# The last feed-forward pass of a fused float32 transformer block: gate and up from parts of 12 significant bits

## The chip, the cores and the metric

The kernel runs on one core of a Trainium2 chip. A core has a matrix engine (TensorE, PE in the profile, with its weight loads as PEld), a vector engine (VectorE, DVE), an activation engine (ScalarE, ACT), a programmable engine (GpSimd, POOL) and a queue engine that here only starts transfers (SyncE, SP). Each engine works through its own instructions strictly in order and waits on semaphores for the others. [...] The metric is the device time of one execution in microseconds (us), the median over runs.

## The reference

Four sequences of 512 rows with 256 features go through a windowed attention, a feed-forward layer, a causal attention and the same feed-forward layer again, each with a residual sum and a row normalization ahead of it. What matters here is the feed-forward layer, whose weights are stored as 4-bit codes with a scale for every 32 of them:

```python
Wg = dequant_nvfp4(gate_W_packed, gate_scales)   # 2048 x 256
Wu = dequant_nvfp4(up_W_packed, up_scales)       # 2048 x 256
Wd = dequant_nvfp4(down_W_packed, down_scales)   # 256 x 2048
gate = jnp.einsum('th,nh->tn', xt, Wg)
up = jnp.einsum('th,nh->tn', xt, Wu)
gelu = jnp.tanh(0.7978845608028654 * (gate + 0.044715 * gate ** 3)) * gate * 0.5 + gate * 0.5
out = jnp.einsum('tn,hn->th', gelu * up, Wd)
...
x = x + attn_a(layernorm(x))
x = x + ffn(layernorm(x))
x = x + attn_b(layernorm(x))
x = x + ffn(layernorm(x))
```

## The kernel before, in words

Everything is float32. The weights are unpacked once, early, and stay in SBUF: `Wf["g"]`, `Wf["u"]` and `Wf["d"]`, each as 2 x 4 tiles of 128 x 512. Index `par` picks the even or odd features (the contraction of 256 is done as two of 128), `q` a quarter of the 2048 hidden units.

A feed-forward pass (`ffn`, from line 891) serves one sequence `b`: 512 columns of activations in `xT` (128 x 2 x 512). It goes through two halves of eight hidden tiles each. For hidden tile n it makes the gate (two matmuls into a PSUM bank `pg`, line 903), on ACT the gelu of it into `gs` (line 915 for passes that use the gelu table, lines 909 to 913 and 930 to 931 for passes beside attention, which build it from a tanh), the up (two matmuls into `pu`, line 924), and on DVE their product `it` (line 935). After eight tiles the down product follows: four row groups `po`, each of eight matmuls over the eight `it` tiles (line 949), and on DVE the sum into the residual `X` (line 964). In the last pass each row group of the second half goes out by DMA (line 971). `pg`, `pu` and `po` share three PSUM banks (pool `fbank`), taken in turn.

There are eight passes, four of the first layer (names ending in f and a digit) and four of the second (s and a digit). `weave` puts the matmuls of a pass by hand between the matmuls of the attention that runs beside it: PE's order is the order written, `tc.manual_schedule(engines=PE_ONLY)`. The order of the instructions on ACT, DVE and POOL isn't written out; the framework's scheduler settles it when the program is built, from its own estimate of when each can run and from the order in which they were created. The pass of sequence 2 (`s2`) is the last with attention beside it. The pass of sequence 3 (`s3`) runs alone at the end of the kernel:

```python
weave(passes(), beside_causal(), 1.0)
weave(ffn(f1, i1, 3, got2[3], "s3", False, True), iter(()), 1.0)
```

Its input `got2[3]` comes from `norm_rows` (line 826): statistics of each row group on DVE (`bn_stats` and `bn_aggr` into `mv`, lines 838 and 839), the inverse root `rs` in two small POOL instructions (`inv_root`, lines 92 and 93: a multiply-add and a power), the normalized rows `xn` on DVE (line 856), eight transposes on PE into `xTp` (line 876), and one ACT copy of 128 x 1024 into `xT` (line 882). In PE's order these eight transposes lie inside the down product of `s2`, after ten of the 32 matmuls of its second half; the other 22 come behind them, and then the gate of `s3`.

The causal attention's tiles lie in four pools (`bc`, `b1`, `b2`, `b4`) that stay open to the end. The last thing the attention does is on POOL: the sum of its output rows into `X` (line 1221).

Of the kernel before, what the change touches and what calls it, by code (L numbers as in the profile page):

```python
# [10 lines left out]
F32 = mybir.dt.float32  # L11
F16 = mybir.dt.float16
I32 = mybir.dt.int32
AF = mybir.ActivationFunctionType
ALU = mybir.AluOpType
AX = mybir.AxisListType

P = 128
B, H, W = 4, 512, 256
# [3 lines left out]
NH = MLP // P  # L23
EPS = 1e-5
MASK = -1e30


def bcast(ap, axis, n):
# [7 lines left out]
def hybrid_kernel(  # L36
# [25 lines left out]
    nc = tc.nc  # L62
# [4 lines left out]
    side = ctx.enter_context(tc.tile_pool(name="ps2", bufs=2, space=bass.MemoryType.PSUM))  # L67
# [818 lines left out]
    def behind_due(ins):  # L886

        if "due" in state:
            queue_behind(ins, state["due"])

    def ffn(pool, ipool, b, xT, name, tanh, last, later=None):
        for half in range(2):
            inter = []
            for n in range(8 * half, 8 * half + 8):
                q, o = n // 4, (n % 4) * P
                if later:
                    later.room()
                    later.want(f"g{q}")
                pg = fbank.tile([P, 512], F32, tag="ps", name=f"pg_{name}_{n}")
                for par in range(2):  # L900
                    if par:
                        yield
                    nc.tensor.matmul(  # L903
                        pg, Wf["g"][par][q][:, o : o + P], xT[:, par, :], start=par == 0, stop=par == 1
                    )
                gs = pool.tile([P, 512], F32, tag="gs", name=f"gs_{name}_{n}")
                if tanh:

                    nc.scalar.copy(gs, pg)  # L909
                    g2 = pool.tile([P, 512], F32, tag="g2", name=f"g2_{name}_{n}")  # L910
                    nc.scalar.activation(g2, gs, AF.Square, scale=0.044715 ** 0.5)  # L911
                    nc.vector.scalar_tensor_tensor(g2, g2, 1.0, gs, ALU.add, ALU.mult)  # L912
                    nc.scalar.activation(g2, g2, AF.Tanh, scale=0.7978845608028654)
                else:
                    nc.scalar.activation(gs, pg, AF.Gelu_apprx_tanh)  # L915
                yield
                if later:
                    later.room()
                    later.want(f"u{q}")
                pu = fbank.tile([P, 512], F32, tag="ps", name=f"pu_{name}_{n}")  # L920
                for par in range(2):
                    if par:
                        yield
                    nc.tensor.matmul(  # L924
                        pu, Wf["u"][par][q][:, o : o + P], xT[:, par, :], start=par == 0, stop=par == 1
                    )
                it = ipool.tile([P, 512], F32, tag="it", name=f"it_{name}_{n}")
                if tanh:
                    gu = pool.tile([P, 512], F32, tag="gu", name=f"gu_{name}_{n}")
                    nc.vector.scalar_tensor_tensor(gu, pu, 0.5, gs, ALU.mult, ALU.mult)  # L930
                    nc.vector.scalar_tensor_tensor(it, g2, 1.0, gu, ALU.add, ALU.mult)
                elif later:
                    later.push(lambda it=it, pu=pu, gs=gs: nc.vector.tensor_tensor(it, pu, gs, ALU.mult), 1.3, 0.6)
                else:
                    behind_due(nc.vector.tensor_tensor(it, pu, gs, ALU.mult))
                inter.append(it)
                yield
            for i in range(4):
                if later:
                    later.room()  # L940
                po = fbank.tile([P, 512], F32, tag="ps", name=f"po_{name}_{half}_{i}")
                for k in range(8):
                    if later and i == 0 and k == 6:
                        later.room(0)
                    if later and i == 0 and k % 4 == 0:
                        later.want(f"d{2 * half + k // 4}")
                    n = 8 * half + k
                    j, par = n // 2, n % 2
                    nc.tensor.matmul(  # L949
                        po[:, 0:W],  # L950
                        inter[k][:, i * P : (i + 1) * P],
                        Wf["d"][par][j // 2][:, (j % 2) * W : (j % 2 + 1) * W],
                        start=k == 0,
                        stop=k == 7,
                    )
                    if k % 2:
                        yield

                parts = 2 if b == B - 1 and last and half == 1 and i == 3 else 1
                for n in range(parts):  # L960
                    at = slice(n * W // parts, (n + 1) * W // parts)

                    def put(i=i, at=at, po=po):
                        return nc.vector.tensor_tensor(X[b][:, i, at], po[:, at], X[b][:, i, at], ALU.add)  # L964

                    if later:
                        later.push(put, 0.4, 0.35)
                    else:
                        behind_due(put())
                    if last and half == 1:  # L970
                        (nc.scalar if n else nc.sync).dma_start(
                            out=out[b, i * P : (i + 1) * P, at], in_=X[b][:, i, at]
                        )

    def causal_consts(bc, c):

# [307 lines left out]
    def weave(main, work, share):  # L1287

        with tc.manual_schedule(engines=PE_ONLY):
            owed = 0.0  # L1290
            for w in work:
                owed += w * share
                while owed >= 0.86:
                    owed -= 0.86
                    next(main, None)
            for _ in main:
                pass
# [305 lines left out]
        for b in range(1, 3):  # L1603
            weave(ffn(f1, i1, b, got[b], f"f{b}", False, False), beside_window(b + 1), 1.0)

    bc = ctx.enter_context(tc.tile_pool(name="bc", bufs=1, side="left"))
    cc, got2 = {}, []

    def passes():
# [4 lines left out]

    def beside_causal():
        yield from causal_consts(bc, cc)
        b1 = ctx.enter_context(tc.tile_pool(name="b1", bufs=1, side="left"))
        b2 = ctx.enter_context(tc.tile_pool(name="b2", bufs=2, side="left"))
        b4 = ctx.enter_context(tc.tile_pool(name="b4", bufs=4, side="left"))
        other = norm_rows(f1, 1, "b1", mine, 5.0, True)  # L1620
        for b in range(B):

            work = scaled(causal_attention(b1, b2, b4, cc, b, mine[b]), 0.8 if b == 0 else 1.045)
            yield from amid(work, other)
            other = causal_end(b)
        yield from other

    weave(passes(), beside_causal(), 1.0)
    weave(ffn(f1, i1, 3, got2[3], "s3", False, True), iter(()), 1.0)


# [86 lines left out]
```

## Time and profile before

| what | value |
|---|---|
| time of the kernel | 1019.37 us median of 3 runs (1018.01 to 1022.12) |
| span of the profiled execution, first to last instruction | 1018.9 us |
| PE busy | 998.9 us, 98% of the span |
| DVE, ACT, POOL busy | 671.3, 351.0, 129.2 us |
| gate of `s3` begins on PE | 932.83 us |
| down of the second half of `s3` begins on PE | 1001.57 us |
| last sums into `X` begin on DVE | 1015.59 us |

No device time is given for the profiled execution by itself; its span is 0.47 us under the median, and inside the three runs. Times in the views are counted in us from the first instruction. A float32 matmul of 128 x 512 leaves two records on PE, so that "x4" in a line of the last pass is the two matmuls of one gate or up tile. The mean length of one such record overlaps the next; the distance from start to start is the true pace. A releaser, as in "<-DVE xn", is what ended the idle time ahead of an instruction.

### The profile page before, as it was taken

The numbers are of one execution on the slowest core, as the hardware profiler recorded it, in microseconds if no ns is written. First come the engines' busy times: TensorE is split into PE (matmuls) and PEld (weight loads), VectorE is DVE, ScalarE is ACT, GpSimd is POOL, SyncE is SP. The second block draws the span as 40 slices with busy tenths as digits, with TensorE's granted clock in tenths as the row PEclk, the third lists the DMA queues.
The fourth block names the chain that finished last, engine by engine and source line by source line (L and its number), as shares of the span: only waits on it lengthen the run. The fifth ranks groups of instructions, "written<-read, shape, count | busy, mean of one in ns | idle before, by whom it ended". The sixth has DMA issues, their size and how long they took to land.

```text
span 1018.9 us, 14266 instructions
## 1 busy us (share of the span) xinstructions
PE 998.9 (98%) x5552; PEld 589.2 (58%) x5552; DVE 671.3 (66%) x1581; ACT 351.0 (34%) x607; POOL 129.2 (13%) x251
## 2 busy tenths in 40 slices
PE   8989998999999999999999999999999999999998
PEld 6864657465746575554574644754645746446556
DVE  8889997987938678756577554766466575652111
ACT  3462142132112223435424346145253253451110
POOL 2100000100000013012330112401113201120000
PEclk9999999999999999999999999999999999999999
DMA  5220100000000020000000000000000000000000
GB/s 157 76 64 22 62 22 13 10 1 1 1 1 1 1 68 1 1 1 1 2 1 0 2 1 1 6 16 1 1 1 1 22 0 2 1 1 21 0 1 21
DMA packets 14900, 15.32 MB, mean 15 GB/s; under 512 B 2866, under 2 KB 11338, under 8 KB 14802
## 3 DMA queue, kind: packets, MB, share of 16 engines
q1 hardware_dynamic: 12416, 13.31, 4.4%
q10 hardware_dynamic: 2322, 1.07, 0.4%
q8 instruction: 43, 0.70, 0.3%
q14 instruction: 23, 0.19, 0.1%
q0 software_dynamic: 96, 0.05, 0.0%
HBM read 12.32 MB, written 2.10 MB: 14 GB/s over the span
## 4 chain that ended last, share of the span: by engine, by line
PE 91%; DVE 5%; ACT 1%; DMA 1%; issue 1%; POOL 0%; SPq 0%; POOLq 0%; DVEq 0%
PE pg_s L903 11%; PE pu_s L924 11%; PE po_s L949 11%; PE pg_f L903 10%; PE pu_f L924 10%; PE po_f L949 10%; PE s L1113 5%; PE o L1198 4%; PE sT L1162 4%; PE qkv_b L1052 3%; PE va L486 2%; PE qkT L1089 1%; PE qkv_b L1056 1%; PE zp L751 1%; PE sc L486 1%; PE ob L1213 1%
## 5 line engine op out<-in xcount | busy, mean ns | idle before, releaser
L1128 DVE CUSTOM_DVE_ANT_0 junk<-s,mask 128x512 f32<-128x512 f32 (+3 forms) x256 | 110.2, 487 | 36.8 <-PE s L1113 19.8
L903 PE MATMUL pg_s<-xT_s,g 128*128 128x512 f32 x256 | 126.7, 603 | 0.0
L924 PE MATMUL pu_s<-xT_s,u 128*128 128x512 f32 x256 | 125.4, 601 | 0.0
L903 PE MATMUL pg_f<-xT_f,g 128*128 128x512 f32 x256 | 123.8, 598 | 0.7 <-ACT xT_f L879 0.7
L924 PE MATMUL pu_f<-xT_f,u 128*128 128x512 f32 x256 | 122.5, 595 | 0.0
L949 PE MATMUL po_s<-d,it_s 128*128 128x256 f32 x512 | 118.0, 382 | 0.0
L949 PE MATMUL po_f<-d,it_f 128*128 128x256 f32 x512 | 117.4, 382 | 0.4 <-DVE d L820 0.4
L949 PEld LDWEIGHTS po_s<-d,it_s 128*128 128x128 f32 x512 | 95.2, 190 | 20.8 <-issue 8.8
L949 PEld LDWEIGHTS po_f<-d,it_f 128*128 128x128 f32 x512 | 95.1, 190 | 18.4 <-issue 5.4
L1178 POOL TENSOR_SCALAR_AFFINE_SELECT e<-e 128x256 f32<-128x256 f32 x128 | 52.5, 422 | 345.2 <-ACT e L1174 342.5
L1174 ACT ACTIVATE e<-sT 128x1024 f32<-128x1024 f32 (+1 forms) x72 | 66.4, 968 | 72.0 <-PE sT L1162 72.0
L924 PEld LDWEIGHTS pu_f<-xT_f,u 128*128 128x128 f32 x256 | 47.3, 190 | 55.0 <-issue 53.0
L903 PEld LDWEIGHTS pg_s<-xT_s,g 128*128 128x128 f32 x256 | 46.0, 190 | 56.8 <-issue 50.9
L915 ACT ACTIVATE gs_f<-pg_f 128x512 f32<-128x512 f32 x48 | 28.6, 596 | 142.2 <-PE pg_f L903 136.5
L924 PEld LDWEIGHTS pu_s<-xT_s,u 128*128 128x128 f32 x256 | 46.1, 190 | 54.4 <-issue 50.2
L903 PEld LDWEIGHTS pg_f<-xT_f,g 128*128 128x128 f32 x256 | 46.8, 190 | 52.8 <-issue 48.1
L912 DVE SCALAR_TENSOR_TENSOR g_s<-g_s,gs_s 128x512 f32<-128x512 f32 x48 | 33.2, 691 | 59.0 <-ACT g_s L911 58.5
L909 ACT COPY gs_s<-pg_s 128x512 f32<-128x512 f32 x48 | 28.1, 586 | 67.8 <-PE pg_s L903 67.6
L1113 PE MATMUL s<-kT,qT 16*128 16x384 f32 (+3 forms) x512 | 50.0, 467 | 0.0
L964 DVE TENSOR_TENSOR X<-po_s,X 128x256 f32<-128x256 f32 (+1 forms) x33 | 13.5, 413 | 54.0 <-PE po_s L949 54.0
L1198 PE MATMUL o<-e,V 128*32 128x256 f32 (+3 forms) x512 | 44.4, 441 | 0.4 <-PE sT L1162 0.4
L1113 PEld LDWEIGHTS s<-kT,qT 16*128 16x128 f32 x512 | 23.1, 183 | 32.5 <-issue 11.6
(241 smaller groups left out, 1348.2 us busy)
## 6 DMA issues: line engine op xcount, KB each, us to landing
X<-in_x_dram SPq DMA_DIRECT2D x4, 512.0 KB
out_dram<-X SPq DMA_DIRECT2D x15, 128.0 KB
xa<-in_x_dram SPq DMA_DIRECT2D x28, 64.0 KB
pkg<-in_gate_p_dram SPq DMA_DIRECT2D x4, 256.0 KB
sbg<-in_gate_s_dram SPq DMA_DIRECT2D x4, 256.0 KB
pku<-in_up_p_dram SPq DMA_DIRECT2D x4, 256.0 KB
sbu<-in_up_s_dram SPq DMA_DIRECT2D x4, 256.0 KB
pkd<-in_down_p_dram SPq DMA_DIRECT2D x4, 256.0 KB
```

The lines of the kernel that those rows point to most:

```text
L486: nc.tensor.matmul(dst, ident, part, start=n == 0 and not onto, stop=n == len(parts) - 1, skip_group_check=onto)
L903: nc.tensor.matmul(pg, Wf["g"][par][q][:, o : o + P], xT[:, par, :], start=par == 0, stop=par == 1)
L912: nc.vector.scalar_tensor_tensor(g2, g2, 1.0, gs, ALU.add, ALU.mult)
L924: nc.tensor.matmul(pu, Wf["u"][par][q][:, o : o + P], xT[:, par, :], start=par == 0, stop=par == 1)
L949: nc.tensor.matmul(po[:, 0:W], inter[k][:, i * P : (i + 1) * P], Wf["d"][par][j // 2][:, (j % 2) * W : (j % 2 + 1) * W], start=k == 0, sto ...
L1052: nc.tensor.matmul(ps[:, 0, :], xT[:, par, rows], c["wqk"][:, :, par], start=par == 0, stop=par == 1)
L1113: nc.tensor.matmul(pss[hl // 2][:, hl % 2, at : at + n], qT[h0 : h0 + HD, g, i * P : (i + 1) * P], kT[h0 : h0 + HD, g, 0:n], start=True, s ...
L1128: nc.vector.tensor_tensor_reduce(out=junk[:, 0:n], in0=pss[k][:, hl % 2, at : at + n], in1=c["mask"][:, 512 - n : 512], scale=1.0, scalar= ...
L1162: nc.tensor.matmul(pss[hl // 2][:, hl % 2, at : at + n], kT[h0 : h0 + HD + 1, g, kt * P : (kt + 1) * P], qT[h0 : h0 + HD + 1, g, kt * P : ...
L1174: nc.scalar.activation(e[:, :, 0 : 512 - at0], pss[k][:, :, at0:512], AF.Exp)
L1178: nc.gpsimd.affine_select(out=diag, in_=diag, pattern=[[0, 2], [1, P]], compare_op=ALU.is_ge, fill=0.0, base=0, channel_multiplier=-1,)
L1198: nc.tensor.matmul(outs[g][h0 : h0 + 32, kt * P : 512], v[:, kt, 4 * g + hl, :], e[:, hl % 2, at : at + n], start=kt == 0, stop=kt == 2,)
```

## The change

In the last pass gate and up are no longer float32 matmuls. Each operand is cut into a top part of 12 significant bits and a remainder, w = w0 + w1 and x = x0 + x1, and held as float32r, the float32 form that by the change's own description PE multiplies in a single pass where float32 takes four. The product needs four terms; the kernel gets them from three products. With s = 2^-12 it sums w0 x0 + w1 (4096 x1), scales that sum by 1 + s in PSUM, and adds (w1 - s w0)(x0 - 4096 x1); written out, this leaves w0 x0 + w0 x1 + w1 x0 + w1 x1. `in_parts` makes the three forms of the activations and `weight_parts` the three forms of each of the 16 gate and up weight tiles:

- activations, per `par`: two ACT instructions (the top part by a rounding scale `NEAR`, and 4096 x) and two DVE instructions
- weights, per tile: the top part on ACT, one form on DVE, the remainder on POOL

The 16 weight triples share 12 buffers, so that those of the last quarter (q = 3) wait until those of the first are used up. All of this lies in a new pool `alone`, which takes the room of the four attention pools; these are closed first.

`ffn_in_parts` replaces `ffn` for `s3`. `begin` does four float32r matmuls into a bank and then scales the bank in place on ACT by 1 + 2^-12; `end` adds two more float32r matmuls to the scaled bank. Between a tile's `begin` and its `end` PE does the `begin` of the next tile. Gelu, product and down (`down`, the old loop moved into a function of its own, line 949 now 956) are as before.

```diff
+F32R = mybir.dt.float32r
+STEP = 2.0 ** -12
+NEAR = 1.0 - 2.0 ** -13
...
+    def in_parts(pool, xT, name):
+
+        x4 = pool.tile([P, 2, 512], F32, name=f"x4_{name}")
+        xs = pool.tile([P, 3, 2, 512], F32R, name=f"xs_{name}")
+        for par in range(2):
+            nc.scalar.activation(xs[:, 0, par], xT[:, par], AF.Copy, scale=NEAR)
+            nc.scalar.activation(x4[:, par], xT[:, par], AF.Copy, scale=4096.0)
+        top = xs.bitcast(F32)
+        for par in range(2):
+            nc.vector.scalar_tensor_tensor(xs[:, 1, par], top[:, 0, par], -4096.0, x4[:, par], ALU.mult, ALU.add)
+            nc.vector.scalar_tensor_tensor(xs[:, 2, par], top[:, 0, par], 4097.0, x4[:, par], ALU.mult, ALU.subtract)
+        return xs
+
+    def weight_parts(pool):
+
+        parts = {}
+        for q in range(4):
+            for mat in ("g", "u"):
+                for par in range(2):
+                    w = Wf[mat][par][q]
+                    t = pool.tile([P, 3, 512], F32R, tag="parts", bufs=12, name=f"w{mat}{par}_{q}")
+                    top = t[:, 0].bitcast(F32)
+                    nc.scalar.activation(t[:, 0], w, AF.Copy, scale=NEAR)
+                    nc.vector.scalar_tensor_tensor(t[:, 2], top, -1.0 - STEP, w, ALU.mult, ALU.add)
+                    nc.gpsimd.tensor_tensor(t[:, 1], w, top, ALU.subtract)
+                    parts[mat, par, q] = t
+        return parts
+
+    def ffn_in_parts(pool, ipool, b, xs, parts, name, last):
+
+        def begin(mat, n):
+            q, o = n // 4, (n % 4) * P
+            ps = fbank.tile([P, 512], F32, tag="ps", name=f"p{mat}_{name}_{n}")
+            for k, (form, par) in enumerate(((0, 0), (0, 1), (1, 0), (1, 1))):
+                nc.tensor.matmul(
+                    ps, parts[mat, par, q][:, form, o : o + P], xs[:, form, par],
+                    start=k == 0, stop=k == 3,
+                )
+            nc.scalar.activation(ps, ps, AF.Copy, scale=1.0 + STEP)
+            return ps
+
+        def end(mat, n, ps):
+            q, o = n // 4, (n % 4) * P
+            for par in range(2):
+                nc.tensor.matmul(
+                    ps, parts[mat, par, q][:, 2, o : o + P], xs[:, 2, par],
+                    start=False, stop=par == 1, skip_group_check=True,
+                )
+            return ps
+
+        for half in range(2):
+            inter, gates, open_ = [], {}, None
+
+            def close():
+                mat, n, ps = open_
+                end(mat, n, ps)
+                if mat == "g":
+                    gs = gates[n] = pool.tile([P, 512], F32, tag="gs", name=f"gs_{name}_{n}")
+                    nc.scalar.activation(gs, ps, AF.Gelu_apprx_tanh)
+                else:
+                    it = ipool.tile([P, 512], F32, tag="it", name=f"it_{name}_{n}")
+                    nc.vector.tensor_tensor(it, ps, gates[n], ALU.mult)
+                    inter.append(it)
+
+            for n in range(8 * half, 8 * half + 8):
+                for mat in ("g", "u"):
+                    ps = begin(mat, n)
+                    yield 0.87
+                    if open_:
+                        close()
+                        yield 0.44
+                    open_ = mat, n, ps
+            close()
+            yield 0.44
+            for _ in down(b, name, half, inter, last):
+                yield 0.87
...
-    bc = ctx.enter_context(tc.tile_pool(name="bc", bufs=1, side="left"))
+    causal = ExitStack()
+    bc = causal.enter_context(tc.tile_pool(name="bc", bufs=1, side="left"))
...
     weave(passes(), beside_causal(), 1.0)
-    weave(ffn(f1, i1, 3, got2[3], "s3", False, True), iter(()), 1.0)
+    causal.close()
+    alone = ctx.enter_context(tc.tile_pool(name="alone", bufs=1, side="left"))
+    xs = in_parts(alone, got2[3], "s3")
+    weave(ffn_in_parts(f1, i1, 3, xs, weight_parts(alone), "s3", True), iter(()), 1.0)
```

In the changed program as built the queues around the start of `s3` run as follows (index of the quarter behind the name; "top" the ACT part of a weight tile, "form" its DVE part, "rest" its POOL part):

```
ACT   tanh of s2's last tile | 12 tops (q 0 to 2) | xT copy | 2 + 2 for x | scale g0 | scale u0 | gelu table load | gelu 0 | scale g1 | scale u1 | gelu 1 ...
      ... scale u3 | tops g q3 x2 | gelu 3 | tops u q3 x2 | scale g4 | scale u4 | gelu 4 ...
DVE   it 15 of s2 | statistics | form g0 | last statistics | form g0 | X sum | xn x4 | forms u0 x2, g1 x2, u1 x2 | X sum | 4 for x | form g2 | X sum | forms g2, u2 x2 | X sum | it 0 ...
POOL  X sum of the attention | rests g0 x2, u0 x2, g1 x1 | rs multiply-add | rest g1 | rs power | rests u1 x2, g2 x2, u2 x2 | rests q3 x4
PE    ... s2 down: 10 matmuls | 8 transposes | 22 matmuls | s3: begin g0, begin u0, end g0, begin g1, end u0, begin u1, end g1 ...
```

More of the change, by code (lines that the diff above doesn't have):

```diff
@@ L937, in ffn @@
                 yield
-            for i in range(4):
-                if later:
[L940 to L954, printed above, removed]
-                    )
[L956 to L973, printed above, removed]
@@ new lines, in ffn, with down, put @@
+            yield from down(b, name, half, inter, last, later)
+    def down(b, name, half, inter, last, later=None):
+        for i in range(4):
+            if later:
+                later.room()
+            po = fbank.tile([P, 512], F32, tag="ps", name=f"po_{name}_{half}_{i}")
+            for k in range(8):
+                if later and i == 0 and k == 6:
+                    later.room(0)
+                if later and i == 0 and k % 4 == 0:
+                    later.want(f"d{2 * half + k // 4}")
+                n = 8 * half + k
+                j, par = n // 2, n % 2
+                nc.tensor.matmul(
+                    po[:, 0:W],
+                    inter[k][:, i * P : (i + 1) * P],
+                    Wf["d"][par][j // 2][:, (j % 2) * W : (j % 2 + 1) * W],
+                    start=k == 0,
+                    stop=k == 7,
+                )
+                if k % 2:
+                    yield
+            parts = 2 if b == B - 1 and last and half == 1 and i == 3 else 1
+            for n in range(parts):
+                at = slice(n * W // parts, (n + 1) * W // parts)
+                def put(i=i, at=at, po=po):
+                    return nc.vector.tensor_tensor(X[b][:, i, at], po[:, at], X[b][:, i, at], ALU.add)
+                if later:
+                    later.push(put, 0.4, 0.35)
+                else:
+                    behind_due(put())
+                if last and half == 1:
+                    (nc.scalar if n else nc.sync).dma_start(
+                        out=out[b, i * P : (i + 1) * P, at], in_=X[b][:, i, at]
+                    )
@@ new lines, in ffn_in_parts @@
+    def ffn_in_parts(pool, ipool, b, xs, parts, name, last):
[12 more added lines that the diff above has]
+            for par in range(2):
+                nc.tensor.matmul(
+                    ps, parts[mat, par, q][:, 2, o : o + P], xs[:, 2, par],
+                    start=False, stop=par == 1, skip_group_check=True,
+                )
+            return ps
[7 more added lines that the diff above has]
+                    nc.scalar.activation(gs, ps, AF.Gelu_apprx_tanh)
+                else:
+                    it = ipool.tile([P, 512], F32, tag="it", name=f"it_{name}_{n}")
[13 more added lines that the diff above has]
+                yield 0.87
@@ L1616, in beside_causal @@
         yield from causal_consts(bc, cc)
-        b1 = ctx.enter_context(tc.tile_pool(name="b1", bufs=1, side="left"))
-        b2 = ctx.enter_context(tc.tile_pool(name="b2", bufs=2, side="left"))
-        b4 = ctx.enter_context(tc.tile_pool(name="b4", bufs=4, side="left"))
+        b1 = causal.enter_context(tc.tile_pool(name="b1", bufs=1, side="left"))
+        b2 = causal.enter_context(tc.tile_pool(name="b2", bufs=2, side="left"))
+        b4 = causal.enter_context(tc.tile_pool(name="b4", bufs=4, side="left"))
         other = norm_rows(f1, 1, "b1", mine, 5.0, True)
```

## The prediction

> **What bounds the kernel now.** I read the chain that ended last first. PE carries nearly all of it:
>
> ```profile
> PE 91%; DVE 5%; ACT 1%; DMA 1%; issue 1%; POOL 0%; SPq 0%; POOLq 0%; DVEq 0%
> ```
>
> Then its pieces in order of time around the start of the last pass (start, length, what):
>
> ```profile
> 917.08 0.74 POOL X L1221
> 917.84 0.75 DVE st_s L838 x2
> ...
> 919.98 0.23 DVE mv_s L839 x2
> 920.28 0.19 POOL rs_s L92
> 920.52 1.07 POOLq L1714
> 921.62 0.42 DVE xn_s L856
> 922.08 1.41 PE xTp_s L876 x8
> 923.49 9.50 PE po_s L949 x44
> 932.99 1.72 PE pg_s L903 x4
> 934.71 1.72 PE pu_s L924 x4
> ```
>
> Two things are to be seen. From 932.99 on, gate and up tiles follow each other every 1.72 us with nothing between: that stretch is PE's alone. And just before it the chain leaves PE: the normalization of sequence 3 goes through two small POOL instructions (the multiply-add and the power of the inverse root, 920.28 to 921.58), and PE's transposes hang on it. PE's order is fixed, so the 22 down matmuls behind the transposes (923.49, 9.50 us) wait as well. That the chain passes through POOL there costs 0.76 us of idle PE, as the timeline says in brackets:
>
> ```profile
> 920.56 1.02 POOL L93 TENSOR_TENSOR rs_s<-rs_s,mhalf 128x4 f32<-128x4 f32 x1
> ...
> 922.08 1.41 PE L876 MATMUL xTp_s<-ident,xn_s 128*128 128x128 f32 x8 [0.76 <-DVE xn_s L856]
> ...
> 924.56 1.28 ACT L915 ACT_TABLE_LOAD   x1
> ```
>
> Last, prices: the instructions of the tile `turned` (min/median/max in ns), and groups by form (busy us, mean ns).
>
> ```profile
> L1071 POOL TENSOR_TENSOR turned<-qb,rt x64: 449/632/645, 385.7 to 800.1; 128x128 f32<-128x128 f32 x64
> ```
>
> ```profile
> L1221 POOL TENSOR_TENSOR X<-X,on 128x256 f32<-128x256 f32 x16 | 11.7, 729 | 32.3 <-DVE on L1219 32.2
> ...
> L911 ACT ACTIVATE g_s<-gs_s 128x512 f32<-128x512 f32 x48 | 30.2, 630 | 1.5
> ...
> L909 ACT COPY gs_s<-pg_s 128x512 f32<-128x512 f32 x48 | 28.1, 586 | 67.8 <-PE pg_s L903 67.6
> ```
>
> **Part 1: fewer passes on PE.** A tile was four records of 0.429 us (1.72). A tile is now six matmuls of 512 columns. No row shows a float32r matmul. The upper bound is the record as it is, 0.429; the lower is half of it, 0.216, since a record of two float32 matmuls' four is two passes. I take 0.216, because the down product shows that PE and its weight loads can keep that pace: 64 records with a new 128 x 128 weight each (its load 0.19) in 13.81 us. So 6 x 0.216 = 1.295 a tile, 0.422 less, and over 32 tiles 13.5 us less.
>
> **Part 2: new waits in the loop.** From the queue order shown above, with 0.20 us from the last column on PE to ACT's start (934.54 to 934.74), 0.60 for a scale or gelu of 128 x 512, and 0.1 back to PE:
> - steady state: a tile's scale is ready 0.9 us after its `begin`, and PE is busy with others for 1.295 until its `end`. ACT's three instructions per n take 1.8 of 2.59 us, DVE's product 0.69. Three banks suffice by some 0.2 us. Nothing is lost. A scale in PSUM in place has no row; between 0.5 and 0.8 us it moves the sum by -0.6 to +1.3.
> - the last `end` of each half has only 0.43 us of cover: 0.49 lost, twice. The first `end` of each half: 0.06, twice.
> - the gelu table load (1.28) lay under s2's down product. Now it stands in ACT's queue behind the scales of tile 0, gelu 0 comes 1.28 later, and `begin` of up 1 needs its bank: 1.04 lost.
> - after n = 3, four tops of 0.63 for q 3 stand between the scales on ACT, two ahead of gelu 3 and two ahead of scale g4: `begin` u4 waits 1.1 for the bank, `end` g4 1.06 for its scale.
>
> Together 4.3 us, so the pass from its first gate to its end gains 13.5 - 4.3 = 9.2 us.
>
> **Part 3: the pass starts later.** This is where the change pays. Five rests are queued on POOL ahead of the multiply-add and a sixth ahead of the power; behind those two stand xn, the transposes, the 22 down matmuls and the whole last pass. The first top can't be used before POOL's sum into X ends (917.81): top at 917.9 to 918.5, first rest at 918.6. A rest of 128 x 512: from 449 ns at 128 columns (the shortest, undisturbed) to 729 at 256 is 2.19 ns a column, so 1.29 us. The bounds are 1.0 (a line from the 468 ns of a POOL product of 128 x 8 through the 729) and 1.46 (twice 729); I take the steeper line, being nearest in shape. Five are 6.45. Beside them DVE runs three instructions with two SBUF inputs (it 15 and two forms); such company stretches POOL from 449 to the median 632, a factor 1.41, over some 3 us: 0.9 more, 925.95. Multiply-add 0.28, rest 1.29, power 1.0: 928.5 where it was 921.58, 6.9 us later. PE, out of work since 921.35, starts the transposes at 929.0 instead of 922.08.
>
> PE has then been idle 7.7 us, and such a gap has a second price. Windows of 1 us show what thin work did early in this run (PE busy 72% of the window 36 to 37, 0.69 us of it idle before; the granted clock is the number after POOL's count):
>
> ```profile
> 38.00:39.00 1.00, 1.00 (x4) 0.74 (x3) 0.97 (x2) 0.00 (x0) 0.92 (x2) 0.50 0.00 0
> 39.00:40.00 1.00, 1.00 (x4) 0.82 (x3) 1.00 (x2) 0.00 (x0) 1.00 (x1) 0.50 0.00 0
> ```
>
> Half clock from about 37.3 to 40.7, so 3.4 us at half speed: 1.6 us lost here. Bounds: nothing, and 2.2 by the 4.36 us that the kernel's very first 20 records took at half pace. [...]
>
> The rest of the preparation hides. The transposes (1.24 us, at half clock 2.5) end at 931.5, their result is on ACT at 931.7; xT copy 1.01 and four ACT parts of 0.63: 935.2. On DVE six forms come first (0.61 apart, stretched by 1.6 beside POOL, as the DVE sum beside `turned` is, 672 ns against 426: to about 935.9), a sum into X, then four parts of x: 939.6. POOL's twelfth rest ends at 938.7. The down product covers all this: it ends at 931.5 + 9.5 + 0.5 (what is left of the half clock's 3.4 us) = 941.5. Without the clock's loss it would end at 939.9, with 0.3 us of cover left. So gate g0 starts at 941.5 against 932.83: 8.6 later. SP's transfers of sequence 2 follow its X sums and are as late; nobody waits for them.
>
> [...]
>
> **Sum.** 1018.9 (the profiled execution's span) - 9.2 + 8.6 = 1018.3. The median of the runs shown is 0.47 above that span: **1018.8 us**, within 0.5% of before (5.1 us, about what a measurement of this kernel can tell from no change). The rest of the kernel is issued as before: the other engines' queues are the same up to s2's last tile.
>
> **Rivals.**
> - *A short delay, faster.* POOL's rests take 1.0 us and don't suffer from DVE, and the clock holds: start 4.4 later, a scale of 0.5 in PSUM: -9.8 + 4.4, 1014.0. For it: the small products' flat line. Against: the 449 and 632. If the root did not wait for the rests at all, the parts of x would set the start, 1.0 late: 1011.2; the queue order speaks against it.
> - *A long delay, slower or the same.* Rests of 1.46 with full blocking and a clock loss of 2.2: POOL's and DVE's forms run one by one, the parts of x come at 944.6 and set the start, 11.9 late: 1022.1. A rest has to take some 2.2 us to pass 1024.5; a POOL path that is slow for float32r output could do that, and no row has one.
> - *The single pass isn't one, slower.* If a float32r matmul costs more than 0.245, 192 of them eat 5.7 us more and the kernel is slower by over 0.5%; at 0.24 it is 1023.4. At 0.429 the pass is 28.1 longer than before, 1056. For it: no row of such a matmul; against: the pace of the down product's loads.
>
> **How the numbers follow.** The balanced case, with its rests between 1.1 and 1.5 and the clock lost or not (1015.5 to 1022), 0.62. Short delay or better, under 1014.3: 0.15. Long delay beyond 1024.5: 0.13. Not a single pass: 0.10, half of it near the threshold. Hence faster 0.15, same 0.62, slower 0.23. The range leaves out a tenth below and a tenth above: 1013.5 to 1025.
>
> **What would show it.** Right: float32r records 0.216 apart; POOL's power ending about 928.5, and PE idle some 7 us ahead of the transposes with a granted clock near 0.5 after them; first gate at about 941.5; from there to the end 77 us against 86; stalls of about 1 us at up 1, twice at tile 4. Wrong: a rest well off 1.3 us, a clock that holds, a pace other than 0.216, or parts of x that arrive behind the down product.

## The result, and the profile after

The changed kernel takes 1025.72 us in the median of 5 runs (1025.27 to 1029.47), beside 1021.74 us for the kernel before in the same comparison (5 runs, 1018.01 to 1022.12). The ratio is 1.0062, 95% interval 1.0043 to 1.0081: slower by 0.6%, where 1018.8 and no measurable change were forecast, and above the range's upper end of 1025.0. The ratio is taken from runs side by side, so it isn't the quotient of the two medians. Before itself stands at 1021.74 here, where the forecast started from 1019.37; about 2 us of scatter lie in any single median. The profiled execution after spans 1026.0 us against 1018.9.

The chain of the changed kernel, its shares by engine. PE has lost a little, DVE holds its 5%, and POOL, which stood at 0%, carries 2%:

```profile
PE 90%; DVE 5%; POOL 2%; ACT 1%; issue 1%; DMA 1%; DVEq 0%; POOLq 0%; SPq 0%; ACTq 0%
```

The pieces of that chain around the start of the last pass (start, length, what):

```profile
918.42 0.74 POOL X L1303
...
919.89 3.52 POOL wg L1007 x2
923.41 2.90 POOL wu L1007 x2
926.31 1.22 POOL wg L1007
...
927.62 0.19 POOL rs_s L96
...
927.89 1.26 POOL wg L1007
929.15 0.99 POOL rs_s L97
930.14 0.03 issue
930.17 5.18 DVE xn_s L860 x4
...
935.39 0.69 PE xTp_s L880 x2
936.08 10.97 PE po_s L956 x44
947.05 0.93 PE pg_s L1017 x4
```

Read against the same stretch before, these are all the losses. This execution was already 1.34 us late when POOL's sum into X began (918.42, before 917.08), ahead of anything that the change touches; that is scatter between executions, and I take it off. Then five rests (919.89 to 927.53), behind them the multiply-add, though its statistics had been ready since 922.38, a sixth rest and the power: the root ends at 930.14, before at 921.58, **7.2 us** later. From the root to the end of the transposes before took 1.91 us (to 923.49) and now takes 5.94 (to 936.08), **4.0 us** more. The 22 down matmuls take 10.97 in place of 9.50, **1.5 us** more. So the first gate starts at 947.05, which is 12.7 us later than before with the 1.34 taken off.

From the first gate to the second half's down product the pass took 68.75 us before (932.99 to 1001.74) and takes 61.77 now (947.05 to 1008.82), **7.0 us** less. In sum 1.34 + 7.22 + 4.03 + 1.47 - 6.98 = 7.1, the whole difference of the two spans.

Where the 4.0 and the 1.5 come from is in the timeline of the changed kernel (start, length, engine, line, tiles, in brackets the idle time before and what ended it):

```profile
930.10 2.54 POOL L1007 TENSOR_TENSOR wu<-u,wu 128x512 fp32r<-128x512 f32 x2
930.17 5.17 DVE L860 TENSOR_SCALAR xn_s<-X,mv_s,rs_s 128x256 f32<-128x256 f32 x4 [5.88 <-POOL rs_s L97]
...
931.57 0.69 PE L880 MATMUL xTp_s<-ident,xn_s 128*128 128x128 f32 x2 [8.90 <-DVE xn_s L860]
932.60 2.58 POOL L1007 TENSOR_TENSOR wg<-g,wg 128x512 fp32r<-128x512 f32 x2
...
932.85 0.69 PE L880 MATMUL xTp_s<-ident,xn_s 128*128 128x128 f32 x2 [0.58 <-DVE xn_s L860]
```

The four normalizations `xn` took 1.38 us before and take 5.17 here, 1.27 from one to the next: the same as POOL's rests, which run beside them 1.27 apart. The holding is one-sided: a rest takes 1.26 undisturbed and hardly more here. And PE, idle for 8.90 us, comes back at half clock. The windows of the changed kernel show it (the granted clock is the number after POOL's count):

```profile
928.00:930.00 2.00, 0.00 (x0) 0.00 (x0) 0.00 (x0) 0.00 (x0) 2.00 (x2) 0.50 0.00 0
...
934.00:936.00 2.00, 1.30 (x5) 0.90 (x6) 2.00 (x3) 0.00 (x0) 2.00 (x2) 0.50 0.00 0
936.00:938.00 2.00, 2.00 (x6) 1.56 (x6) 2.00 (x2) 1.85 (x3) 2.00 (x2) 0.50 0.00 0
938.00:940.00 2.00, 2.00 (x9) 1.68 (x8) 2.00 (x4) 1.35 (x3) 0.14 (x1) 0.77 0.00 0
940.00:942.00 2.00, 2.00 (x11) 1.77 (x10) 2.00 (x5) 0.00 (x0) 0.00 (x0) 1.00 0.00 0
```

The transposes, one pair in 1.27 us, didn't bring the clock back. Only the dense down product from 936.08 on did, after some 2.8 us by the mean of 0.77 in the window from 938 to 940.

Inside the pass the chain shows the pace and the waits:

```profile
949.55 1.28 ACT L1041
...
950.84 0.61 ACT gs_s L1041
...
951.49 1.20 PE pu_s L1017 x4
...
953.15 0.91 PE pg_s L1017 x4
954.06 0.45 PE pu_s L1027 x2
954.51 0.91 PE pu_s L1017 x4
```

Six float32r matmuls take 1.36 us from 953.15 to 954.51, 0.2268 each at full clock; 192 of them are 43.5 us. Gate and up together take 61.77 - 13.81 = 47.96, so 4.4 us are waits, the first of them that of up 1 (951.49) for gelu 0, which has the load of its table ahead of it (949.55). A wait costs more than its idle time: the four matmuls behind this one take 1.20 in place of 0.91, and behind each of the other waits of the pass it is the same 0.28 or so. Up 1, up 4, the end of gate 4, gate 5 and the two half ends stand idle for 2.5 us together, and six such restarts add 1.7.

### The profile page after: what moved, and what is told of

The parts are those of the page before. It is cut to its first block, busy times and chain, and to the rows that moved or that the text cites. A ratio compares the mean times of both kernels' runs of the same rounds, so it can differ in the third digit from the quotient of the medians.

```text
span 1026.0 us, 14507 instructions
## 1 busy us (share of the span) xinstructions
PE 993.7 (97%) x5616; PEld 602.3 (59%) x5616; DVE 692.6 (68%) x1601; ACT 379.0 (37%) x659; POOL 153.2 (15%) x267
## 4 chain that ended last, share of the span: by engine, by line
PE 90%; DVE 5%; POOL 2%; ACT 1%; issue 1%; DMA 1%; DVEq 0%; POOLq 0%; SPq 0%; ACTq 0%
PE po_s L956 11%; PE pg_f L907 10%; PE pu_f L928 10%; PE po_f L956 10%; PE pg_s L907 9%; PE pu_s L928 8%; PE s L1195 5%; PE o L1280 4%; PE sT L1244 4%; PE qkv_b L1134 3%; PE va L490 2%; PE qkT L1171 1%; PE pu_s L1017 1%; PE pg_s L1017 1%; PE qkv_b L1138 1%; PE zp L755 1%
## 5 line engine op out<-in xcount | busy, mean ns | idle before, releaser
L907 PE MATMUL pg_s<-xT_s,g 128*128 128x512 f32 x192 | 96.6, 607 | 0.0
L928 PE MATMUL pu_s<-xT_s,u 128*128 128x512 f32 x192 | 95.3, 604 | 0.0
L907 PEld LDWEIGHTS pg_s<-xT_s,g 128*128 128x128 f32 x192 | 33.8, 189 | 42.4 <-issue 36.5
L928 PEld LDWEIGHTS pu_s<-xT_s,u 128*128 128x128 f32 x192 | 34.0, 190 | 39.1 <-issue 34.9
L971 DVE TENSOR_TENSOR X<-po_s,X 128x256 f32<-128x256 f32 (+1 forms) x33 | 13.5, 411 | 45.6 <-PE po_s L956 45.6
L1153 POOL TENSOR_TENSOR turned<-qb,rt 128x128 f32<-128x128 f32 x64 | 35.2, 578 | 50.2 <-DVE qb L1142 33.4
```

What stands on the lines that cost most here:

```text
L907: nc.tensor.matmul(pg, Wf["g"][par][q][:, o : o + P], xT[:, par, :], start=par == 0, stop=par == 1)
L928: nc.tensor.matmul(pu, Wf["u"][par][q][:, o : o + P], xT[:, par, :], start=par == 0, stop=par == 1)
L1153: nc.gpsimd.tensor_tensor(turned[:, :, half], qb[:, kind, :, 8 - 8 * half : 16 - 8 * half], bcast(sin[:, 8 * half : 8 * half + 8], 1, HEAD ...
```

## The experiments

The theory after this reading had two parts. *Blocking*: a DVE instruction and a rest on POOL don't run side by side but one by one, so that 12 rests and 16 DVE instructions ahead of the pass are one serial chain. *Queue*: rests stand ahead of the root, so everything behind it waits. The rivals were that the pass itself brings less than thought (pace and waits), and that the amount of preparation is too much for any engine.

Executions differ in when the attention ends, by a few us, so I compare traces by one stretch: from the start of POOL's last attention sum into X to the start of the second half's down product. `queue_behind(a, b)` places an instruction behind another in its engine's queue, without a wait.

| run | stretch, us | against before | median, us | ratio and interval |
|---|---|---|---|---|
| before | 84.66 | | | |
| changed kernel | 90.40 | +5.7 | 1025.72 | 1.0062, 1.0043 to 1.0081 |
| parts made, not used | 99.28 | +14.6 | 1033.26 | 1.0110, 1.0084 to 1.0136 |
| root first | 87.12 | +2.5 | 1022.48 | 1.0017, 1.0001 to 1.0033 |
| xn first | 88.84 | +4.2 | 1024.80 | 1.0046, 1.0026 to 1.0066 |
| xn first, x early, two more | 87.52 | +2.9 | 1022.83 | 1.0019, 1.0000 to 1.0039 |
| rests on DVE | 81.90 | -2.8 | 1017.19 | 0.9969, 0.9951 to 0.9987 |
| spread, rests on POOL | 76.87 | -7.8 | 1013.12 | 0.9938, 0.9920 to 0.9957 |
| spread, rests on DVE | 75.44 | -9.2 | 1012.58 | 0.9937, 0.9920 to 0.9954 |
| the same again | 75.38 | -9.3 | 1011.14 | 0.9915, 0.9896 to 0.9934 |
| and two down matmuls first | 74.57 | -10.1 | 1009.52 | 0.9902, 0.9886 to 0.9917 |

The kernel before took 1021.74 us in the median beside the changed kernel, 1019.79 beside the four runs below it, 1020.22 beside the next three and 1020.58 beside the last two; each ratio is taken from runs side by side. In the last row the rest of the down product is counted from where it would have begun in one piece.

**The preparation alone.** The old float32 pass, with all parts made beside it and left unused.

```diff
-    weave(ffn_in_parts(f1, i1, 3, xs, weight_parts(alone), "s3", True), iter(()), 1.0)
+    weight_parts(alone)
+    weave(ffn(f1, i1, 3, got2[3], "s3", False, True), iter(()), 1.0)
```

> The preparation alone: all parts of weights and of x are made as in the changed kernel, but the last pass runs the old float32 loop and nothing reads the parts. Theory Q (POOL's rests stand ahead of the inverse root and hold up xn, then the clock): the first gate of the last pass starts about 12.7 us later than before, so about 12.7 us over the kernel before (11 to 15). Rival L (the loss is in the new loop: pace, refill, table load): within 2 us of the kernel before.

Measured: 1033.26, 13.5 over the median of before; first gate at 944.44 with X's sum at 915.33, 13.2 later than before counted from that sum. The preparation by itself costs more than the pass can win. Whatever the pass brings, the loss is here. The run is not quite the changed kernel's preparation: as nothing reads the parts, the last quarter's four weights are made ahead of the pass too, 16 instead of 12.

**Another order.** First the rests queued behind the root's power:

```diff
-                    nc.gpsimd.tensor_tensor(t[:, 1], w, top, ALU.subtract)
+                    rest = nc.gpsimd.tensor_tensor(t[:, 1], w, top, ALU.subtract)
+                    queue_behind(rest, state["root s3"])
```

> One part undone: on POOL the rests are queued behind the root's power instead of ahead of it; nothing else. Theory Q: POOL's power ends some 1.5 us after the last statistics, as before the change, 7 us earlier than in the changed kernel; xn still runs beside rests, 1.27 us each, so the transposes end about 4 us later than before; six blocked forms then keep the parts of x back. 3 to 6 us under the changed kernel, that is from 2 under to 1 over the kernel before. If the place in the queue were all there is to the late start: 12 us under the changed kernel. Rival L: no difference from the changed kernel (4 us over the kernel before).

Measured: 1022.48. The root ends at 920.63, 5.4 after X's sum began where it was 4.5 before, so the 7.2 are down to 0.9. But `xn` takes 5.18 us all the same, and the transposes behind it again leave PE at a granted clock of 0.50 in the window from 926 to 930. Then the rests, made to wait by a semaphore for the last `xn`:

```diff
-                    nc.gpsimd.tensor_tensor(t[:, 1], w, top, ALU.subtract)
+                    rest = nc.gpsimd.tensor_tensor(t[:, 1], w, top, ALU.subtract)
+                    tc.add_manual_dep(
+                        rest.ins, state["s3"],
+                        mybir.DependencyInfo(mybir.DependencyClass.Sync, mybir.DependencyReason.DATA),
+                        reason="after xn",
+                    )
```

> As e1, and the rests also wait (by semaphore) until the four xn are done, so that no rest runs beside them. Theory Q with the port: xn take 0.41 us each again, PE waits under 1 us for the transposes, the clock holds at 1.0, the down product ends about 933; what is late next is the parts of x behind six forms, each stretched to some 1.7 us beside a rest: first gate at about 940, 2 to 4 us under the kernel before. If nothing is late next: 7 us under the kernel before. Rival L: no difference from the changed kernel.

Measured: 1024.80. (The port of the expectation is the blocking; no run shows its cause.) Now `xn` takes 1.39, the transposes end at 921.6 and the down product at 931.0: the way to the pass is 0.7 to 0.9 late and no more. Yet the run is 4.2 us over before in the stretch, where 2 to 4 under were expected. The timeline of this run shows what PE meets there:

```profile
931.42 1.75 DVE L993 SCALAR_TENSOR_TENSOR xs_s<-xs_s,x_s 128x512 fp32r<-128x512 f32 x1
...
933.10 1.74 DVE L992 SCALAR_TENSOR_TENSOR xs_s<-xs_s,x_s 128x512 fp32r<-128x512 f32 x1
...
934.25 3.38 POOL L1007 TENSOR_TENSOR wg<-g,wg 128x512 fp32r<-128x512 f32 x2
...
934.99 0.47 PE L1022 MATMUL pg_s<-xs_s,wg 128*128 128x512 f32 x1 [2.87 <-DVE xs_s L992]
...
938.57 2.08 PE L1022 MATMUL pu_s<-xs_s,wu 128*128 128x512 f32 x4 [3.12 <-DVE X L971]
...
943.14 2.08 PE L1022 MATMUL pg_s<-xs_s,wg 128*128 128x512 f32 x4 [1.64 <-DVE X L971]
```

A part of x that takes 0.68 us by itself takes 1.75 beside the rests, 1.68 from one to the next. The fourth matmul of the first gate waits for it. Up 0 and gate 1 then wait for something the prediction had not looked at: the sums of s2's down product into X (L971), which free the three PSUM banks that the matmuls write into, and stand in DVE's queue between forms. These gaps of 2.87 and 3.12 us cost the clock as well: it stands at 0.72 in the window from 934 to 938 and at 0.50 in the two from 938 to 946, where four matmuls take 2.08 us, though PE is busy for 2.93 us of the four from 938 to 942. Nothing on record had foreseen that for this run.

Third, the same with x's parts ahead of all weights but the first quarter's, gelu's table loaded early, and the last quarter's parts under the first half's down product:

```diff
+    queue_behind(nc.scalar.activation(early, mhalf, AF.Gelu_apprx_tanh), state["x"]["act"])
...
+            if half == 0:
+                weight_parts(alone, parts, (3,), after)
```

> e2, and: the parts of x are queued on ACT and DVE ahead of the tops and forms of quarters 1 and 2; the gelu table is loaded under the down product; the parts of quarter 3 are made under the down product of the first half. Theory Q: first gate within 2 us of the kernel before, no stall at up 1 nor at tile 4, the pass some 9.7 us shorter than before at 0.227 us a matmul: 7 to 10 us under the kernel before. Rival L: the two loop stalls gone are worth 3 us against the changed kernel, so about 1 over the kernel before.

Measured: 1022.83, in the stretch 2.9 over before where 7 to 10 under were expected. Gate 0 starts at 931.71, counted from X's sum 0.7 later than before the change. But gate 1 starts at 943.51, having waited 4.96 for a DVE sum. In the three orders gate 1 starts at 943.61, 943.14 and 943.51. Moving the work in the queues only moves the place where PE waits: the serial chain of DVE and POOL work from about 918 to 943 is as long in each. In this one too the clock fell, to 0.50 from about 937 to 947 (0.86 in the windows 934 to 938 and 946 to 950, 0.50 in the two between), which costs some 1.9 us behind 943.51 (2.08, 0.85 and 1.31 us in the chain in place of 0.93, 0.47 and 0.93). The waits inside the pass are all but gone in this run, and yet it is no faster than before the change.

**One engine instead of two.** The decisive edit is one word, with the order as in the changed kernel:

```diff
-                    nc.gpsimd.tensor_tensor(t[:, 1], w, top, ALU.subtract)
+                    nc.vector.tensor_tensor(t[:, 1], w, top, ALU.subtract)
```

> The rests go to DVE and POOL has none; nothing else changes, the forms and parts of x stand in the same queue order. Blocking theory (DVE instructions with two SBUF inputs and POOL's rests stop one another whole, so that the preparation ran one by one for 25 us): 28 instructions of 0.61 on DVE alone take 17 us, POOL's multiply-add and power come on time, first gate at about 933, no half clock. DVE's queue still holds ten instructions ahead of the first product, so the third tile waits for its bank until about 944.7: the end comes 2 to 5 us under before, about 1015 to 1018. Rival (the amount of the preparation sets the start, whichever engine does it): DVE as the only engine is later still, 943 or more for tile 1, 1022 to 1026 as in the runs with another order.

Measured: 1017.19, ratio 0.9969, some 8.5 us under the changed kernel, though DVE now does all the forms and rests that two engines shared. The timeline of this run:

```profile
922.29 1.38 DVE L860 TENSOR_SCALAR xn_s<-X,mv_s,rs_s 128x256 f32<-128x256 f32 x4 [1.19 <-POOL rs_s L97]
...
922.76 1.41 PE L880 MATMUL xTp_s<-ident,xn_s 128*128 128x128 f32 x8 [1.64 <-DVE xn_s L860]
...
932.27 0.68 DVE L1006 SCALAR_TENSOR_TENSOR wg<-wg,g 128x512 fp32r<-128x512 f32 x1
932.87 0.68 DVE L1007 TENSOR_TENSOR wg<-g,wg 128x512 fp32r<-128x512 f32 x1
933.48 0.69 DVE L1006 SCALAR_TENSOR_TENSOR wg<-wg,g 128x512 fp32r<-128x512 f32 x1
...
942.21 1.19 PE L1017 MATMUL pg_s<-xs_s,wg 128*128 128x512 f32 x4 [0.78 <-ACT gs_s L1041]
```

Form and rest follow each other every 0.60 us, 1.20 for a pair. Beside POOL a pair took 1.68. A second engine made the work slower, not faster: that is the blocking, and the rival "too much preparation" falls. It isn't wholly one by one, since a rest of 1.22 and a form of 0.60 alone would make 1.82. Two details went otherwise than expected. First gate came at 935.35, not 933: the root was 0.9 late, with one form (0.57) ahead of the last statistics and the multiply-add stretched to 0.54 from 0.19 beside DVE's next instruction, and the down product took 11.19, at a granted clock of 0.61 and 0.54 in the windows 924 to 926 and 926 to 928, after an idle gap of just 1.64 us. The xn-first run had the same gap of 1.64 there and kept full clock. And the wait for a bank was at up 1 and gate 2, 0.7 to 0.8 us each, not one long wait at 944.7.

**Less at a time.** The version that follows from this: only the first quarter's parts are made ahead of the pass, and those of the other three in the loop, two weights behind each product of tiles 0, 1, 4, 5, 8 and 9; gelu's table is loaded early. `weight_parts` here takes the quarters and matrices to make, and the ACT and DVE instructions (`after`: the last gelu, the last product) behind which they are queued.

```diff
+    quarter0 = weight_parts(alone, {}, (0,), {"dve": state["s3"]}, ("g",))
     xs = in_parts(alone, got2[3], "s3")
...
                     inter.append(it)
+                    q = n // 4 + 1
+                    if n < 12 and n % 4 in (0, 1):
+                        weight_parts(alone, parts, (q,), after, ("gu"[n % 4],))
```

Once with the rests on DVE, ahead of their forms:

> Rests on DVE, only the first quarter's parts made ahead of the pass (two weights ahead of the parts of x, two behind), every other quarter's made in the loop behind earlier products and gelus, gelu's table loaded under the down product. Blocking and queue theory: first gate at 933 to 934 as before the change, no half clock, the pass from there to the end 72.2 (75.6 as measured less the stalls of 3.4 that this takes out), so 9 to 10 us under before: 1009 to 1012. Rival (the pass itself brings less, since its pace falls or the parts on ACT and DVE hold the scales and products up in the loop): start at 933 to 934 all the same, but the pass at 75 or more, 1013 to 1016.

and once with the rests on POOL, the first four waiting for `xn`:

> The same with the rests on POOL, those of the first quarter held until xn is done. If blocking costs only where much of it stands ahead of the pass: four rests of 1.29 and eight DVE instructions of 0.61 one by one, 10.3 us from 923.0, with X sums between: first gate at 934 to 935, 1010 to 1013. Rival (any rest on POOL beside DVE is dear, in the loop too: products wait behind forms that wait for rests): tiles 1 to 10 stall by some tenths each, 1014 to 1018.

Measured: 1012.58 and 1013.12, ratios 0.9937 and 0.9938; the first lies just outside its 1009 to 1012, since the pass took 73.4 us in place of 72.2. The first again with more rounds:

> The best version once more, with more rounds, for the interval. Its profile showed the pass 9.2 us shorter and starting no later: 1010.5 to 1013.

Measured: 1011.14, ratio 0.9915. The chain of that run around the start of the pass has no preparation in it at all:

```profile
915.91 0.74 POOL X L1310
...
920.92 1.41 PE xTp_s L880 x8
922.33 9.50 PE po_s L956 x44
931.83 0.93 PE pg_s L1021 x4
```

From X's sum to the first gate it takes 15.92 us, before the change 15.91. The version with POOL is 1.4 us longer in the stretch. There two forms beside rests take 2.87 us (from 940.26), the product of tile 2 comes behind them at 943.05, and gate 4 waits 0.37 for its bank, as gate 12 does later. So rests on POOL are bearable where little else is queued on DVE; the damage came from 12 of them at once, ahead of the pass.

Last, the waits at the half ends, by two matmuls of the down product ahead of the last `end`:

```diff
-            close()
+            rows = down(b, name, half, inter, last)
+            next(rows)
+            yield 0.87
+            close()
```

> The best version with the first two matmuls of each half's down product ahead of the last end. Prices the half ends: PE has 0.86 us of work where it waited 0.28 and 0.3 for the last scale, twice, so 0.9 to 1.2 us under the best version. Rival (the product of tile 7 comes no sooner, and the down product waits for it in the same measure at its eighth matmul): the same as the best version within 0.3.

Measured: 1009.52, ratio 0.9902 (0.9886 to 0.9917), the fastest version of the study. In the traces it is 0.8 us shorter than the one without, a little under the expected 0.9 to 1.2.

**Prices.** Single runs, read by their traces alone. The refill of the last quarter (edit as above, nothing else changed):

> The changed kernel with the last quarter's parts made under the first half's down product. Prices the refill: up 4 and the end of gate 4 no longer wait behind tops, nor gate 5 behind forms. Theory (the loop's waits are as foreseen in size): the pass from its first gate to its last down product is 1.6 us shorter than in the changed kernel, 2.2 by the prediction's sum. Rival (the waits only move to tiles 12 to 15): no shorter.

Measured: from first gate to the second down 59.73 in place of 61.77, so 2.0 us (948.69 to 1008.42). Its three waits stood idle for 1.2 us; three restarts of 0.28 make up the rest.

The table load:

> The changed kernel with gelu's table loaded behind the parts of x, under the down product. Prices the load in the loop: up 1 no longer waits 0.74 us, the pass is 0.9 us shorter (1.04 by the prediction's sum). Rival (the load only changes place with another wait for gelu 0): under 0.3.

Measured: the pass is only 0.2 us shorter. But from the start of up 0 to that of up 1 it takes 2.80 in place of 3.50, and with the restart behind the wait, to the end of gate 1, 3.73 in place of 4.69: 1.0 less, about the 1.04 of the forecast. The gain was eaten by another pace: 0.93 and 0.47 us where the changed kernel has 0.91 and 0.45, 0.2333 for a matmul, which makes 1.2 us over 192. So the load's own price is 1.0, and the miss is a second effect.

The pace by columns:

```diff
-            for k, (form, par) in enumerate(((0, 0), (0, 1), (1, 0), (1, 1))):
-                nc.tensor.matmul(
-                    ps, parts[mat, par, q][:, form, o : o + P], xs[:, form, par],
-                    start=k == 0, stop=k == 3,
-                )
+            for h in range(0, 512, 256):
+                for k, (form, par) in enumerate(((0, 0), (0, 1), (1, 0), (1, 1))):
+                    nc.tensor.matmul(
+                        ps[:, h : h + 256], parts[mat, par, q][:, form, o : o + P], xs[:, form, par, h : h + 256],
+                        start=k == 0, stop=k == 3,
+                    )
```

> The version with the rests on DVE, each of the four products of a beginning split into two of 256 columns. If the 0.2268 us of a 128x512 float32r matmul is 0.2133 (half of the float32 record's 0.4263 less nothing, that is 512 columns at full clock) and a fixed 0.0135 for each instruction, two halves take 0.240 in place of 0.2268 and 128 of them cost 1.7 us more. If the pace is by the column alone, nothing more: 0.1134 each. If the weights' load sets the pace at 256 columns, 0.19 each, 19 us more.

A `begin` split like this no longer gives the right gate and up, so the run serves the pace alone. It is built on the spread version with the rests on DVE. The chain:

```profile
938.22 0.94 PE pg_s L1022 x8
939.16 0.47 PE pu_s L1032 x2
939.63 0.94 PE pu_s L1022 x8
```

Eight of 256 columns take 0.94, so 0.1175 each. But this run's own matmuls of 512 columns, in an `end`, take 0.47 for two, 0.235 each, and not the 0.2268 of the changed kernel. Within the run two halves cost the same as one whole, so the pace is by the column, and a fixed part of some 13.5 ns for each instruction is not there. Why the whole run goes at 0.235 it doesn't say.

Where the parts lie, by an unused tile ahead of them:

```diff
+    pad = alone.tile([P, 8], F32, name="pad")
+    nc.gpsimd.memset(pad, 0.0)
```

> The best version with an unused tile of 32 bytes a partition allocated ahead of the parts, so that they lie 32 bytes further. In two runs that allocate such a tile ahead of the weights' parts (for the early load of gelu's table) four float32r products took 0.93 us, in all others 0.91. Theory (the place of the weights' parts in SBUF sets this): 0.93 here, so 1.2 us more over the pass's 192 products. Rival (it is a scatter from execution to execution, or comes from the early load): 0.91.

> The same with 64 bytes. If an offset of 32 bytes makes the slower pace because tiles then straddle units of 64: 0.91 here. If any other place than the first one is slower: 0.93. By the rival 0.91 in both.

Measured: 0.91 for four in both. A shift of the parts by 32 or 64 bytes does nothing. Why three runs went at the slower pace (the table load early in otherwise the old order, the third order above, and the halves) stays open.

## Why the prediction was wrong

Taken against its own sum, the prediction had the profiled execution 0.6 us under before, and it came out 5.7 over after the 1.3 us of scatter: 6.3 us of error. By its parts:

- **Part 3, the root behind the rests: right.** Forecast 6.9 later, measured 7.2. The price of a rest (1.29) was 1.22 to 1.26 undisturbed, and the order, five ahead of the multiply-add and one ahead of the power, is in the chain as told.
- **Part 3, from the root to PE's down matmuls: wrong, 2.9 us.** The step "PE, out of work since 921.35, starts the transposes at 929.0" let `xn` run as before. It needs 5.17 us beside the rests that follow the root. The forecast had looked at what stands ahead of the root on POOL, and not at what stands behind it. This is the step that failed most.
- **Part 3, the clock: the loss right, size wrong, 1.0 us.** PE fell to half clock, as said. That a gap of 7.7 us would cost it was an estimate from rows with a gap of 0.69; the one of 8.90 did. But the forecast counted 3.4 us from the first transpose. The half clock lasted to about 939, 7 us from the first transpose, and took 1.5 us of the down product in place of 0.5. In the rows from which the 3.4 came PE was busy without a pause (1.00 of each us from 38 to 40). The transposes, 0.69 us of work in every 1.27, left the clock at 0.50 to their end, and not only because they were transposes: in the xn-first run float32r matmuls that filled 2.93 of the four us from 938 to 942 left it there too. The dense down product had it back after some 2.8 us. This difference between thin and dense work the forecast left out.
- **Part 3, "the rest of the preparation hides": right in effect, wrong in time.** The last part of x was done at 943.83, 2.9 us later than told once the scatter is off, and the down product covered it only because that was itself late, to 947.05. The three other orders show what it costs when it isn't: 943 is then the start of gate 1.
- **Part 3, the stretching: the wrong choice.** The sum stretched the forms by 1.6 and POOL by 1.41, by the row of `turned`. In the runs a form or a part of x starts every 1.68 us beside rests, 0.60 alone, and a rest alone takes 1.22: all but 0.15 of the two lengths one after the other. The row of `turned` was misread: in the trace before, beside `turned` DVE works on instructions that read two tiles of SBUF, and one of each starts every 0.595 us, where alone they start about 0.41 and 0.34 apart. That is the sum less the same 0.15. Whole durations overlap from one instruction to the next (a form of 0.68 us is followed after 0.60), so stretched durations were no sign that the two engines share; the forecast took blocking for sharing. `xn`, with one tile of SBUF as input and two columns of scalars, is held as well, 1.27 in place of 0.345.
- **Part 1, the pace: right kind, mis-sized by 2.1 us.** A float32r matmul of 128 x 512 took 0.2268 us where a float32 one takes two records of 0.429, a factor of 3.8. That is near one pass in place of four, but the runs show the times alone and count no passes. And it was 0.2268, not 0.216: 43.5 us for 192 where 41.4 were counted. The 0.216 was half a record, and the pace of a down record, whose output is 128 x 256; no run shows why the float32r matmul takes 0.011 more.
- **Part 2, the waits: right.** 4.4 us against 4.3; by single terms, the refill 2.0 against 2.2, the table 1.0 against 1.04, the half ends 1.1 against 0.98, of which two down matmuls ahead won 0.8 back.

So the first gate came 4.1 us later than forecast and the pass won 2.2 less. Of the rivals the long delay is nearest: full blocking and a clock loss were its mechanism, but it put the decision at the parts of x, when it lay at `xn`. The forecast of about half a record for a matmul held, and "wrong if the parts of x arrive behind the down product" didn't happen here, only in the reordered runs.

What stays open is why `xn` is held: the runs show that it is (5.17 and 5.18 us beside rests, 1.38 to 1.39 in every run without rests beside it), not by which of its reads or writes.

## What to carry to other kernels

Two engines that block one another are worse than one: form and rest took 1.20 us on DVE and 1.68 shared with POOL, so try the single queue first. When work is added ahead of a chain, list not only what stands before each of its links on every queue, but also what runs beside them, and what in those queues frees PSUM banks. And preparation that is needed late belongs behind the first tiles that can run without it. The same arithmetic went from 0.6% slower to 1.0% faster, by several edits together: the rests on DVE alone, the parts made a quarter at a time inside the loop, the table loaded early and the last `end` of each half covered. To tell sharing from blocking, compare the distance from start to start alone and together; durations overlap, and added up they hide it.

## What the runs showed of the hardware

- Four rests of 128 x 512 on POOL held a one-input DVE instruction of 128 x 256 for their whole length each: 1.27 us from one to the next, 0.345 without them. The rests themselves went from 1.22 to 1.26 undisturbed to 1.27.
- A form (two SBUF inputs, 128 x 512) on DVE and a rest on POOL took 1.68 us a pair, against 0.60 and 1.22 alone; on DVE alone a pair took 1.20.
- An idle gap of 8.90 us left PE at a granted clock of 0.50, and four pairs of transposes 1.27 us apart left it there; behind 936.08 the dense down product brought it back after some 2.8 us. In the three reordered runs it stood at 0.50 behind gaps of 2.59 us (root first, 926 to 930), 2.87 and 3.12 (xn first, 938 to 946), and 3.22 and 4.96 (the third order, 938 to 946). A gap of 1.64 us cost the clock in one run (down product 11.19 us) and not in another (9.50).
- A float32r matmul of 512 columns with new weights took 0.2268 us. In three runs it was 0.233 to 0.235, with the first half's down product at 13.81 us as in the changed kernel, for a reason not found; in one of them one of 256 columns took 0.1175, half of that.
- Each wait of PE in the loop cost about 0.28 us beyond its idle time: the four matmuls behind it took 1.20 in place of 0.91.
